# Copies moved, v's weights joined, key sums halved and TensorE kept busy at the start of an attention and FFN layer

## The chip, the cores and the metric

The kernel runs on one NeuronCore of a Trainium2 chip. The metric is the device time of one execution in microseconds. An engine is a unit of the core with an instruction queue of its own: TensorE (PE; its weight loads are PEld), VectorE (DVE), ScalarE (ACT), GpSimd (POOL), and SyncE (SP), which here only issues transfers. Transfers are also issued by POOL; those of POOL go into one queue and those of SP into another, and both are served by the same 16 DMA engines.

## The reference

```python
x = x + attn(layernorm(x))     # 2 x 2048 rows of 1024; one head of 256
x = x + ffn(layernorm(x))
# attn: q, k, v = x @ Wqkv + bqkv;  softmax(q k^T / 16) v;  @ Wo + bo
# ffn:  h = relu(x @ up_w) ** 2;  shared = h @ down_w
#       routed = ((x @ fc1_w) @ expert_w * (sum of the top 2 of x @ gate_w)) @ fc2_w
#       layernorm(shared + routed) * ln_gamma + ln_beta
```

up_w is 1024 x 2048, down_w 2048 x 1024, fc1_w 1024 x 512, expert_w 512 x 512, fc2_w 512 x 1024; all is fp32.

## The kernel before, in words

The 4096 rows are eight blocks of 512. Every fp32 operand of a product is split into a high and a low part, and a product is three matmuls: high x high, low x high, high x low. `Pass3` (line 130) issues them, so nearly all of TensorE's work has the line L130. A `split` (L142, L143) is a ScalarE copy for the high part and a VectorE (at times POOL) subtraction for the low part.

**Start** (`begin`, L458 and on). expert_w (tile `ew`) is loaded in four column pieces and transposed on TensorE (`pt`, L480); then fc2_w, the first rows of x and Wqkv are loaded by SP. expert_w and fc2_w are multiplied together once (`pf`, `fold`), in two halves; between the parts of the second half the first block's rows are transposed.

**Projections** (`qkv_block`, L408). For each block TensorE computes v in four tiles of 128 rows (`pv`, 3 x 8 matmuls of 256 columns each) and then q and k in four groups (`pq`, 24 matmuls of 512 columns). Blocks 4 to 7 come first, then 0 to 3. During a block the rows of the next one are normalised, transposed on VectorE within 32 x 32 squares (`xblk`, L213), written to memory (`xt_d`, L218) and fetched in another order (`xt`, L224), both by POOL, and split. The fourth tile is split by the next block (`x3`). q goes to memory (`q_d`), as k and v of blocks 4 to 7 do. The order here is the program's own (`manual_schedule`).

**Attention** (L715 to L775). In the loop over n, TensorE interleaves scores of block n (`ps`) with values of block n-1 (`po`). ScalarE copies scores out of PSUM, VectorE keeps their maximum; `row_max` transposes it; `softmax` subtracts, takes exp, splits, and adds each pair of key chunks into a tile `sum` of two halves of 512 columns. `finish` copies the output out (`o`) and sums over keys with one-column matmuls (`psum`, L622): two for each of four row tiles, which the profile counts as 16. `project` (L632) multiplies with Wo (`pw`) and adds the residual `xres`, which SP loads and to which POOL adds bo with an accumulating transfer (L638). A scheduler orders this part on each engine, and its order need not be the program's.

**FFN** (from L1033, in the program's own order). Each of four pairs of blocks runs an up stage (`pu`, with fc1_w beside up_w) and a down stage (`pd`, with the folded fc2 beside down_w), by a scheme of Strassen's kind: seven products p1 to p7 of quarters instead of eight, ten weight pieces each. The right factors are the quarters (0,0), (1,0), (1,1) of a weight matrix and four sums of quarters. `sum_step` (L387) makes them in memory by POOL's transfers during projections and attention: it copies the quarter, or the first term of a sum, and adds further terms with accumulating transfers. `stage`, `cast_piece` and `end_piece` load a piece (`w`, L810), make its high part on ScalarE (L833) and its low part on VectorE (L841), about two pieces ahead of TensorE; pieces that are used again are stored (`w_p`, L844). `Norm.step` normalises the second block of the first pair during the first up stage, group by group; `split_x` splits it for p4.

Of the kernel before, what the change touches and what calls it, by code (L numbers as in the profile page):

```python
# [17 lines left out]
P = 128  # L18
# [7 lines left out]
def kernel(  # L26
# [184 lines left out]
    def transpose_write(r, q=nc.gpsimd):  # L211
# [7 lines left out]
        return d  # L219

    def fetch_tile(d, q=nc.gpsimd):

        xt = row("xt")
        q.dma_start(  # L224
            out=xt.rearrange("p (a f) -> p a f", a=P // SQ),
            in_=d.rearrange("(a i) (q f) -> (i q) a f", i=SQ, q=P // SQ),
        )
        return xt
# [150 lines left out]


    FIRST = {1: (0, 1), 2: (1, 1), 3: (0, 1), 4: (1, 0)}
    SUMS = [(s, q) for s in range(2) for q in (1, 3, 2, 4)]
    COPIES = SUMS + [(s, q) for s in range(2) for q in ((0, 0), (1, 0), (1, 1))]
    ADDS = dict(zip((4, 5, 6, 8, 9, 10, 11, 13), SUMS))
    last = [None]

    def sum_step(i):  # L387

        s, q = COPIES[i]
        for o, t in zip(sum_tile(s, q), quarter(s, *FIRST.get(q, q))):  # L390
            nc.gpsimd.dma_start(out=o, in_=t)
        if i in ADDS:
            s, q = ADDS[i]
            if q % 2:
                terms = quarter(s, *((0, 0) if q == 1 else (1, 1)))
            else:
                terms = sum_tile(s, q // 2)
            for o, t in zip(sum_tile(s, q), terms):
                nc.gpsimd.dma_start(out=o, in_=t, accum_op=ALU.add, max_dma_last_dim=4096)

# [7 lines left out]
    def qkv_block(n, wqkv, xT, parts, after):  # L408

        keep = n < BPB
        units = {a: (unit if n == BPB - 1 else ex_unit)(f"{a}{n}") for a in "kv"}
        if keep:
            kv[n] = [units["k"], units["v"]]
        got = {}

        def v_tile(t):
            pm = bank(psa, "pv")
            if t % 2 == 0:  # L420
                got["v"] = half("v")
            acc = Pass3(pm[:, :D], NCC)
            for c in range(NCC):
                acc.add(x_chunk(xT, c, ts(t, P)), piece(wqkv[2], c, D, slice(0, D)))
            vt = got["v"][:, ts(t % 2, D)]
            nc.vector.tensor_tensor(vt, pm[:, :D], bv_sb, ALU.add)
            flush()
            split_late(vt, *(hl(units["v"])[:, s, ts(t, D)] for s in range(2)))

        def qk_chunk(a, dc):  # L430
            i = "qk".index(a)
            pm = bank(psa, "pq")
            acc = Pass3(pm, NCC)
            for c in range(NCC):
                acc.add(piece(wqkv[i], c, D, ts(dc, P)), x_chunk(xT, c))
            bias = bqk_sb[:, i * NDC + dc : i * NDC + dc + 1]
            flush()
            if a == "q":
                if dc == 0:
                    got["q"] = row("q")  # L440
                nc.scalar.activation(got["q"][:, ts(dc, W)], pm, AF.Identity, bias=bias)
            else:
                h, l = (hl(units[a])[:, s, ts(dc, W)] for s in range(2))
                nc.scalar.activation(h, pm, AF.Identity, bias=bias)
                nc.vector.scalar_tensor_tensor(l, pm, bias, f32(h), ALU.add, ALU.subtract)

        for j, (a, i) in enumerate(parts):
            v_tile(i) if a == "v" else qk_chunk(a, i)
            if (a, i) == ("q", NDC - 1):
                nc.gpsimd.dma_start(out=q_d[n], in_=got["q"])  # L450
            after(j)
        flush()
        if not keep:
            for a, d in (("k", k_d), ("v", v_d)):
                nc.gpsimd.dma_start(out=d[n], in_=f32(units[a]))

    order = list(range(BPB, NBLK)) + list(range(BPB))
    def begin(wqkv, xT):  # L458
# [15 lines left out]
        nc.gpsimd.dma_start(out=bv_sb, in_=bqkv[2 * D : 3 * D].partition_broadcast(P))  # L474

        eh, el = unit("eh"), unit("el")
        for mc in range(NLC):
            pt = bank(psc, "pt")
            for lc in range(NLC):
                nc.tensor.transpose(pt[:, ts(lc, P)], ew[:, ds(lc * LAT + mc * P, P)], ident)  # L480
            split(pt, eh[:, ts(mc, LAT)], el[:, ts(mc, LAT)])

        def split_f2(h, eng):
# [24 lines left out]
        for t in range(NB):  # L508
            if t + 1 < NB:
                stats.append(row_stats(first[t + 1]))  # L510
            normalise(first[t], stats[t])
            if t == 0:
                f2hl = split_f2(1, nc.gpsimd)
            elif t == 2:
                wqkv[2] = split_unit(*ws[2], nc.gpsimd)
        r = [folded(0, accs)]
        r.append(folded(1, fold(f2hl, lambda t: transpose_tile(first[t], t, xT))))
        wqkv[0] = split_unit(*ws[0])
# [48 lines left out]
    def row_max(n):  # L567
# [5 lines left out]
        m4 = small.tile([P, NB], FP, tag="m4", name="m4")  # L573
        nc.vector.tensor_reduce(m4, pt.rearrange("p (t k) -> p t k", k=P), AX.X, ALU.max)
        s["mb"] = bank(psc, "pmb")
        for t in range(NB):
# [4 lines left out]
    def softmax(n, j):  # L581
# [5 lines left out]
        e2 = e.rearrange("p (k n) -> p k n", n=W)  # L587
        mb = s["mb"].unsqueeze(1).to_broadcast([P, 2, W])
        nc.vector.tensor_tensor(e2, e2, mb, ALU.subtract)
        nc.scalar.activation(e, e, AF.Exp, scale=SC)  # L590
# [3 lines left out]
        elif j == 1:  # L594
            s["sum"] = row(f"sum{n}")
            nc.vector.tensor_tensor(s["sum"], s["e0"], e, ALU.add)
        else:
            nc.vector.tensor_tensor(s["sum"], s["sum"], e, ALU.add)

# [11 lines left out]
    def finish(n):  # L611
# [8 lines left out]
        for t in range(NB):  # L620
            for i in range(2):
                nc.tensor.matmul(  # L622
                    pt[:, t : t + 1],
                    lhsT=s["sum"][:, ds(i * W + t * P, P)],
                    rhs=ones,
                    start=i == 0,
                    stop=i == 1,
                )
        s["ri"] = small.tile([P, NB], FP, tag="ri", name="ri")
# [28 lines left out]
    def a_block(i, norm, xT, x3):  # L658
# [5 lines left out]
        def after(j):  # L664
            if i + 1 == NBLK:
                if j == 0:
                    x3()
                elif j == 2 * NB - 1:
                    start(0, load_row(q_d[0]))
                    for k in range(NKC):  # L670
                        scores(0, k)
                    start(1, load_row(q_d[1]))
                    row_max(0)
# [17 lines left out]
    wqkv, xT = {}, new_xT("a")  # L691
    with tc.manual_schedule():
        norm, fold = begin(wqkv, xT)
        x3 = lambda: None
        steps = list(range(len(COPIES)))
        for i in range(NBLK - 1):
            norm, xT, x3 = a_block(i, norm, xT, x3)
            if i == 0:
                for h in range(C // W):
                    nc.gpsimd.dma_start(  # L700
                        out=cols(fc2e, h, W), in_=fold[h].rearrange("p (c n) -> p c n", n=W)
                    )
            if i >= NBLK // 2:
                sum_step(steps.pop(0))
    a_block(NBLK - 1, None, xT, x3)

    wo_f = [load_row(Wo[ts(dc, P), :]) for dc in range(NDC)]

# [3 lines left out]
    for n in range(1, NBLK + 1):  # L712
# [4 lines left out]
        for k in range(NKC + lag):  # L717
# [23 lines left out]
            elif n == NBLK:  # L741
                if k < NB:
                    xts[k] = fetch_tile(xts[k], nc.sync)
                elif k % 2 == 0 and k >= 6 and k < 6 + 2 * NB:
                    split_x(xts, 0, k // 2 - 3, X["p1"])
            if k in (2, 8) and n > 1 and steps:
                with tc.issue_after(last[0].ins):
# [37 lines left out]

    UPS = [up_order(4 if b == 0 else 1) for b in range(NBLK // 2)]
    DOWN = [(p, i) for p in ("p1", "p2", "p6", "p5", "p3", "p7", "p4") for i in range(NK)]
# [4 lines left out]

    def source(s, q, i):
        t, j = (tsum[s, q][0], i) if i < HU // P else (tsum[s, q][1], i - HU // P)
        return t[:, ts(j, P)].rearrange("(c p) i -> p c i", p=P) if s == 0 else t[ts(j, P), :]

    def stage():
# [3 lines left out]
        if len(pieces) < LATE and early:  # L801
            staged.append((early.pop(0), False, None))
            return
        n_w[0] += 1
        w = (wk if n_w[0] % 7 else wv).tile([P, 2 * W], FR, tag="w", name="w")
        if (s, p, i) in kept:
            nc.sync.dma_start(out=w.bitcast(FP), in_=kept[s, p, i])
            staged.append((w, False, None))
            return
        nc.sync.dma_start(out=as_piece(f32(w)[:, W : 2 * W], s), in_=source(s, RIGHT[p], i))  # L810

# [4 lines left out]
        else:  # L816
            keep = b == 1 or i % 2 == 0
        staged.append((w, True, (s, p, i) if keep else None))

# [9 lines left out]
    def cast_piece():  # L829

        w, raw, key = staged.pop(0)
        if raw:
            nc.scalar.copy(w[:, 0:W], f32(w)[:, W : 2 * W])  # L833
        cast.append((w, raw, key))

    def end_piece():

        w, raw, key = cast.pop(0)
        if raw:
            v = f32(w)  # L840
            nc.vector.tensor_tensor(w[:, W : 2 * W], v[:, W : 2 * W], v[:, 0:W], ALU.subtract)  # L841
        if key:
# [190 lines left out]
    with tc.manual_schedule():  # L1033
        for b in range(NBB):
# [72 lines left out]
            for m, (p, i) in enumerate(UPS[b]):  # L1107
# [46 lines left out]
                if m % 2 and m < 17:  # L1154
                    out_step()
                if b == 0 and m in (0, 1, 2, 4, 6, 8, 9, 10, 11, 12, 13):
                    norm2.step()
                if b == 0 and m < NB:
                    split_x(x_t[0], 1, m, X["p2"], split_late)

                m4 = 12 if b == 0 else 10
                if m == m4:
# [174 lines left out]
```

## Time and profile before

| what | us |
|---|---|
| median of three runs | 2361.1 (2359.96 to 2361.95) |
| the profiled execution | 2357.94 |
| its span, from the first instruction to the last | 2355.8 |
| TensorE busy in the span | 2323.3 |
| VectorE busy | 1501.8 |
| ScalarE busy | 1168.1 |
| POOL busy | 285.4 |

The stages in the profiled execution: the start to 39 us, projections to 304, the first scores from there on, attention to about 776, then four pairs of up and down stages. The last matmul ends near 2342. Bytes moved are 572.54 MB in all.

In the page, a busy row gives tenths in 40 equal slices of the span, some 59 us each; PEclk is the TensorE clock granted, DMA the mean busy share of the 16 engines. A line of the chain of waits reads: start, duration, and what the time belongs to, with a count. A line of a timeline reads: start, duration, engine, line and operation, out<-in, shape and count, and in brackets the idle time before it with what ended it. Busy times of matmuls overlap, so their spacing is taken from the chain or from successive starts.

### The profile page before, as it was taken

The numbers are of one execution on the slowest core, as the hardware profiler recorded it, in microseconds if no ns is written. First come the engines' busy times: TensorE is split into PE (matmuls) and PEld (weight loads), VectorE is DVE, ScalarE is ACT, GpSimd is POOL, SyncE is SP. The second block draws the span as 40 slices with busy tenths as digits, with TensorE's granted clock in tenths as the row PEclk, the third lists the DMA queues.
The fourth block names the chain that finished last, engine by engine and source line by source line (L and its number), as shares of the span: only waits on it lengthen the run. The fifth ranks groups of instructions, "written<-read, shape, count | busy, mean of one in ns | idle before, by whom it ended". The sixth has DMA issues, their size and how long they took to land.

```text
span 2355.8 us, 29360 instructions
## 1 busy us (share of the span) xinstructions
PE 2323.3 (99%) x10704; PEld 1919.4 (81%) x10704; DVE 1501.8 (64%) x2238; ACT 1168.1 (50%) x1916; POOL 285.4 (12%) x425
## 2 busy tenths in 40 slices
PE   8999999999999999999999999999999999999997
PEld 7888888888887778788788888878888877888886
DVE  5566559888877575797645577753456683435656
ACT  6555455555544643667552374743055564214245
POOL 3232111011110110111110011110000021000001
PEclk9999999999999999999999999999999999999999
DMA  5977884999997766786897789786567589665674
GB/s 197 318 256 276 286 205 127 296 315 323 286 253 211 250 208 191 228 276 209 265 316 242 229 297 319 229 267 227 193 204 278 194 267 331 189 191 187 204 247 134
DMA packets 222208, 572.54 MB, mean 243 GB/s; under 512 B 18368, under 2 KB 80320, under 8 KB 220016
## 3 DMA queue, kind: packets, MB, share of 16 engines
q1 hardware_dynamic: 152160, 315.67, 39.9%
q0 software_dynamic: 69904, 255.00, 36.1%
q8 instruction: 85, 1.39, 0.2%
q14 instruction: 59, 0.48, 0.1%
HBM read 430.61 MB, written 197.66 MB: 267 GB/s over the span
## 4 chain that ended last, share of the span: by engine, by line
PE 91%; DMA 3%; issue 3%; DVE 1%; ACT 1%; POOL 0%; SPq 0%; POOLq 0%; DVEq 0%; ACTq 0%
PE pu L130 31%; PE pd L130 28%; PE po L130 7%; PE pq L130 7%; PE ps L130 7%; PE pv L130 4%; PE pw L130 4%; DMA w<-wt 2%; PE pg L890 1%; PE pf L130 1%; PE psum L622 1%; DMA xt<-xt_d 0%; DVE w L841 0%; DMA ew<-in_L_ffn_expert_w_dram 0%; DMA res<-x 0%
## 5 line engine op out<-in xcount | busy, mean ns | idle before, releaser
L130 PE MATMUL pd<-w,sp 128*128 128x512 f32 x3336 | 759.0, 389 | 4.9 <-DVE y L1274 4.8
L130 PEld LDWEIGHTS pd<-w,sp 128*128 128x128 f32 x3336 | 625.5, 188 | 137.3 <-ACT nm L260 6.0
L130 PE MATMUL pu<-xh,w 128*128 128x512 f32 x2240 | 692.8, 390 | 0.1
L130 PEld LDWEIGHTS pu<-xh,w 128*128 128x128 f32 x2240 | 419.2, 188 | 89.9 <-DVE w L841 1.5
L130 PE MATMUL pu<-xl,w 128*128 128x512 f32 x1120 | 436.2, 389 | 0.9 <-DVE xl L150 0.9
L841 DVE TENSOR_TENSOR w<-w 128x512 fp32r<-128x512 f32 x280 | 191.6, 687 | 99.0 <-ACT w L833 92.0
L833 ACT CAST w<-w 128x512 fp32r<-128x512 f32 x280 | 170.9, 615 | 166.2 <-DMA w<-wt 155.6
L130 PEld LDWEIGHTS pu<-xl,w 128*128 128x128 f32 x1120 | 210.2, 188 | 45.1 <-DVE xl L150 1.4
L1077 ACT CAST sp<-h 128x512 fp32r<-128x512 f32 x238 | 146.3, 618 | 151.9 <-PE pd L130 125.6
L1082 DVE TENSOR_TENSOR sp<-h,sp 128x512 fp32r<-128x512 f32 x238 | 162.9, 687 | 68.1 <-ACT sp L1077 67.9
L130 PE MATMUL po<-p,v 128*128 128x512 f32 x768 | 194.3, 391 | 0.6 <-DVE p L143 0.6
L130 PE MATMUL ps<-q,k 128*128 128x512 f32 x768 | 192.5, 390 | 1.5 <-DVE max L565 1.5
L130 PEld LDWEIGHTS ps<-q,k 128*128 128x128 f32 x768 | 143.6, 188 | 31.8 <-DVE max L565 1.9
L130 PEld LDWEIGHTS po<-p,v 128*128 128x128 f32 x768 | 143.0, 188 | 30.2 <-DVE p L143 1.0
L150 DVE TENSOR_TENSOR xl<-xt,xh 128x512 fp32r<-128x512 f32 x108 | 74.4, 689 | 134.9 <-ACT xh L149 134.9
L1027 ACT ACTIVATE h<-h 128x1024 f32<-128x1024 f32 x48 | 50.7, 1055 | 208.8 <-DVE h L1137 159.8
L560 ACT COPY s<-ps 128x512 f32<-128x512 f32 x128 | 75.0, 587 | 133.5 <-PE ps L130 133.4
L213 DVE STREAM_TRANSPOSE xblk<-xrow 128x1024 f32<-128x1024 f32 x60 | 121.1, 2018 | 9.6 <-ACT xrow L283 9.6
L844 POOL DMA_DIRECT2D w_p<-w x115 | 61.6, 536 | 508.7 <-DVE w L841 435.0
L565 DVE TENSOR_TENSOR max<-ps,max 128x512 f32<-128x512 f32 x120 | 82.4, 687 | 36.3 <-ACT s L560 36.1
L130 PE MATMUL pq<-xha,w_h 128*128 128x512 f32 x256 | 99.7, 389 | 0.0
L130 PE MATMUL pq<-xha,w_l 128*128 128x512 f32 x256 | 99.7, 389 | 0.0
(181 smaller groups left out, 3031.8 us busy)
## 6 DMA issues: line engine op xcount, KB each, us to landing
w<-w_p SPq DMA_DIRECT2D x280, 512.0 KB, 4.2
w<-wt SPq DMA_DIRECT2D x280, 256.0 KB, 3.4
w_p<-w POOLq DMA_DIRECT2D x115, 512.0 KB, 4.6
xt_d<-xblk POOLq DMA_DIRECT2D x56, 512.0 KB, 4.4
xt<-xt_d POOLq DMA_DIRECT2D x56, 512.0 KB, 6.7
wt<-in_L_ffn_up_w_dram POOLq DMA_DIRECT2D x9, 2048.0 KB, 23.8
wt<-in_L_ffn_down_w_dram POOLq DMA_DIRECT2D x9, 2048.0 KB, 31.1
xres<-in_L_attn_x_dram SPq DMA_DIRECT2D x32, 512.0 KB, 11.2
```

The costliest lines, as they stand in the source:

```text
L130: nc.tensor.matmul(self.ps, lhsT=a, rhs=b, start=self.i == 0, stop=self.i == self.n - 1, skip_group_check=self.on,)
L150: late_ops.append(lambda: nc.vector.tensor_tensor(lo, t, f32(hi), ALU.subtract))
L213: nc.vector.transpose(b.rearrange("p (q k i) -> p q k i", q=P // SQ, i=SQ), r.rearrange("p (k i q) -> p q k i", k=NCC, i=SQ),)
L560: nc.scalar.copy(s["s"][k // 4][:, ts(k % 4, W)], pm)
L565: nc.vector.tensor_tensor(s["max"], pm, s["max"], ALU.max)
L622: nc.tensor.matmul(pt[:, t : t + 1], lhsT=s["sum"][:, ds(i * W + t * P, P)], rhs=ones, start=i == 0, stop=i == 1,)
L833: nc.scalar.copy(w[:, 0:W], f32(w)[:, W : 2 * W])
L841: nc.vector.tensor_tensor(w[:, W : 2 * W], v[:, W : 2 * W], v[:, 0:W], ALU.subtract)
L844: nc.gpsimd.dma_start(out=kept[key], in_=w.bitcast(FP))
L1027: nc.scalar.activation(o, v, AF.Relu)
L1077: nc.scalar.copy(t[:, 0:W], v)
L1082: add(t[:, W : 2 * W], v, f32(t)[:, 0:W], ALU.subtract)
```

## The change

- `v_tile`: the high and low parts of v's weights lie side by side in one tile, so the high part of x is multiplied with both in one matmul of 512 columns, and the low part of x with the high part in one of 256. VectorE adds the two halves of the result. `begin` splits these weights in two parts, later than before.
- `softmax`: ahead of the last pair of key chunks the two halves of `sum` are added, and the last pair is added in two steps of 512; `finish` then needs one matmul for each row tile.
- `begin`: 3, 14 and 5 transposes of the identity into a spare bank, before, amid and after the transposes of expert_w.
- `sum_step`: only sums are made in it, with the steps in a new order (17 of them, a copy and an addition each a step). One step is issued in `begin`, one after block 4 of the projections (i == 4), three after the maximum of attention block 0 (behind a small POOL addition that reads it), the others two for each n from 2 to 7. The down stage's plain quarters are copied by `copy_step`: (0,0) after i == 5, (1,0) and (1,1) in 20 pieces during the first up stage. The up stage's plain quarters are read from up_w and fc1_w directly into another buffer (`raw`), except for the first four pieces, of which a copy `lead` is made.
- Loads of the first two q rows and of Wo go from SP's queue to POOL's, behind the last fetch of the projections.
- In the first up stage the second block's normalisation runs at m = 0, 1, 2, 3, 4, 6, 7, 8, 9, 10, 11 (before: 0, 1, 2, 4, 6, 8 to 13), and its split starts at m = 11 instead of 13.

```diff
+    FIRST = {1: (0, 1), 2: (1, 1), 3: (0, 1), 4: (1, 0)}
+    SECOND = {1: (0, 0), 2: 1, 3: (1, 1), 4: 2}
     SUMS = [(s, q) for s in range(2) for q in (1, 3, 2, 4)]
-    COPIES = SUMS + [(s, q) for s in range(2) for q in ((0, 0), (1, 0), (1, 1))]
-    ADDS = dict(zip((4, 5, 6, 8, 9, 10, 11, 13), SUMS))
+    STEPS = [(a, 0) for a in SUMS[:3]]
+    for a, c in zip(SUMS, SUMS[3:] + [None] * 3):
+        STEPS += ([(c, 0)] if c else []) + [(a, 1)]
+    STEPS.insert(3, None)
...
+    def copy_step(q, part=None):
+
+        for j, (o, t) in enumerate(zip(sum_tile(1, q), quarter(1, *q))):
+            if part is None:
+                nc.gpsimd.dma_start(out=o, in_=t)
+            elif part // (HU // P) == j:
+                i = ts(part % (HU // P), P)
+                nc.gpsimd.dma_start(out=o[i, :], in_=t[i, :])
...
-                acc.add(x_chunk(xT, c, ts(t, P)), piece(wqkv[2], c, D, slice(0, D)))
+                xh, xl = x_chunk(xT, c, ts(t, P))
+                w = wqkv[2][c // 4].rearrange("p (c n) -> p c n", n=2 * D)[:, c % 4]
+                ops = [(pm, xh, w), (pm[:, :D], xl, w[:, :D])]
...
+            nc.vector.tensor_tensor(vt, pm[:, D : 2 * D], vt, ALU.add)
...
+        busy(3)
         for mc in range(NLC):
+            if mc == 2:
+                busy(14)
...
+        busy(5)
...
+        if n == 0:
+
+            mark = small.tile([P, NB], FP, tag="mark", name="mark")
+            after = nc.gpsimd.tensor_tensor(mark, m4, m4, ALU.add)
+            with tc.issue_after(after.ins):
+                for _ in range(3):
+                    sum_step(steps.pop(0))
...
+        if last:
+            half_sum = s["sum"][:, 0:W]
+            nc.vector.tensor_tensor(half_sum, half_sum, s["sum"][:, W:C], ALU.add)
...
+            for i in range(2):
+                nc.vector.tensor_tensor(half_sum, half_sum, e[:, ts(i, W)], ALU.add)
...
+    with tc.issue_after(fetched[0].ins):
+        q_rows = [load_row(q_d[i], nc.gpsimd) for i in range(2)]
     a_block(NBLK - 1, None, xT, x3)
 
-    wo_f = [load_row(Wo[ts(dc, P), :]) for dc in range(NDC)]
+    with tc.issue_after(fetched[0].ins):
+        wo_f = [load_row(Wo[ts(dc, P), :], nc.gpsimd) for dc in range(NDC)]
...
+    def direct(s, p, i):
+
+        return s == 0 and p in ("p1", "p2", "p3") and (p, i // LEAD) != ("p1", 0)
...
+        if direct(s, p, i):
+            raw = spp.tile([P, 2 * W], FP, tag="sp", name="raw")[:, 0:W]
+        else:
+            raw = f32(w)[:, W : 2 * W]
+        nc.sync.dma_start(out=as_piece(raw, s), in_=source(s, p, i))
...
-                if b == 0 and m in (0, 1, 2, 4, 6, 8, 9, 10, 11, 12, 13):
+                if b == 0 and m in (0, 1, 2, 3, 4, 6, 7, 8, 9, 10, 11):
                     norm2.step()
...
-                m4 = 12 if b == 0 else 10
+                if b == 0 and m % 2 == 0 and 14 <= m < 14 + 4 * NK:
+                    j = m // 2 - 7
+                    copy_step((1, j // NK), j % NK)
+
+                m4 = 10
```

## The prediction

> **What bounds the kernel now.** I read the page first, to see which engine has no slack.
>
> ```profile
> span 2355.8 us, 29360 instructions
> ...
> PE 2323.3 (99%) x10704; PEld 1919.4 (81%) x10704; DVE 1501.8 (64%) x2238; ACT 1168.1 (50%) x1916; POOL 285.4 (12%) x425
> ...
> PEclk9999999999999999999999999999999999999999
> DMA  5977884999997766786897789786567589665674
> ```
>
> TensorE is busy 99% of the span; everything else has slack on average, though DMA stands at 9 from slice 7 to 11, the attention stage. So the time is the sum of TensorE's spacings plus its few gaps, and an edit counts by what it does to one or the other. The spacing of matmuls comes from the chain of waits, which here is TensorE itself:
>
> ```profile
> 39.43 11.51 PE pv L130 x96
> 50.94 21.79 PE pq L130 x96
> ...
> 378.89 1.68 PE psum L622 x16
> ```
>
> A v group of 256 columns follows its predecessor by 11.51/96 = 120 ns, a q/k group of 512 by 21.79/96 = 227 ns, a one-column sum over keys by 1.68/16 = 105 ns. Then the gaps: in the order of TensorE's starts I looked for every step longer than its kind's usual one. The start first (timeline of TensorE):
>
> ```profile
> 3.67 1.94 PE L480 MATMUL pt<-ident,ew 128*128 128x128 f32 x8 [3.67 <-DMA ew<-in_L_ffn_expert_w_dram]
> 9.11 1.94 PE L480 MATMUL pt<-ident,ew 128*128 128x128 f32 x8 [3.49 <-DMA ew<-in_L_ffn_expert_w_dram]
> 12.24 0.79 PE L130 MATMUL pf<-f2h,eh 128*128 128x512 f32 x1 [1.19 <-ACT f2h L142]
> ```
>
> Seven starts from 12.24 on lie about 427 ns apart instead of 227; only at 15.57 does the clock record show the full clock. The largest gap is at the last block of the projections (chain of waits, 266 to 282 us):
>
> ```profile
> 268.85 1.69 issue
> 270.54 7.66 DMA xt<-xt_d
> ...
> 278.23 0.63 ACT xha L142
> ```
>
> The last transposed tile lands at 278.2 and TensorE, at its v group, loses 2.39 + 0.86 = 3.25 us; the clock record then shows half clock from 281.81 for 3.41 us, another 1.6 us. The other gaps: 1.65 us at 712 and 1.09 us at 832; three of 1.3 to 2.2 us at the ends of the down stages (1138, 1530, 1922) and the 13 us after the last matmul, which the change leaves alone. The one at 712 starts here (timeline of ScalarE):
>
> ```profile
> 705.64 0.59 ACT L560 COPY s<-ps 128x512 f32<-128x512 f32 x1 [2.13 <-PE ps L130]
> 711.90 0.62 ACT L833 CAST w<-w 128x512 fp32r<-128x512 f32 x1 [5.66 <-DMA w<-wt]
> ```
>
> ScalarE stands 5.66 us for the first FFN weights, the score copies queue behind it, and a score group waits for its bank.
>
> **The change part by part**, against the profiled execution's 2357.94 us (span 2355.8, 2.1 around it). The median of the runs, 2361.1, is 3.2 above that; I take the difference to the median.
>
> *v's weights side by side.* Per tile and chunk three groups of 256 (3 x 120 = 360 ns) become one of 512 and one of 256 (227 + 120 = 347). 8 blocks x 4 tiles x 8 chunks = 256 times 13 ns = **-3.3 us**, all on the path. The Trainium skill ("TensorE: Matmul & The Clock Gate", Back-to-back issue gap) speaks against it: warm spacing is columns/2.4 plus only 2.5 ns, so joining two groups would save 256 x 2.5 = 0.6 us. The rows show 2 x 120 - 227 = 13 ns of fixed cost per group in this kernel, and I take the rows. VectorE gets 32 more additions of 128x256 from PSUM, 0.42 us each by the v row (13.4 us in eight 33 us blocks in which it is some 60% busy): hidden under TensorE; a v bank is held 0.4 us longer of four, 2.8 us apart: nothing. Without that cover it would be 13 us. The hi and lo halves of the v weights now come from two POOL subtractions of half size (4.62 us by the row at 26.59, so 2.3 each), ending near 34, before the first v group near 36.5: nothing.
>
> *Sums over keys halved.* 8 of 16 one-column passes per finish go: 8 blocks x 8 x 105 ns = 6.7 us. That time also covered the copies of the attention output that the projection needs. In the finishes at 378 to 666, VectorE's chain itself waits 1.2 us for these sums, so it moves up with them, and TensorE has five to seven score groups in between: full gain. At 725 the second half of the output ends at 727.3 and is needed at 727.4; there I give back 0.4. **-6.3 us**. VectorE pays three additions of 512 (0.69 each) for one of 1024 (1.2) per block, +0.9 of 57 us at 83% load: hidden, and not in the last stretch before the sums.
>
> *Kept awake.* 3 + 14 + 5 transposes of the identity. At 243 ns cold (1.94/8) the 14 fill 3.4 of the 3.49 us before 9.11. TensorE is then busy from about 3 to 12, so it should be at full clock at 12.2: the cold excess of 0.37 + 6 x 0.20 = 1.57 us goes, and the last eight transposes take 109 instead of 243 ns, of which the landing of the last weights and VectorE's first low half leave some 0.4. **-2.0 us**. Ends: 0 if such transposes don't count as activity, -2.6 if nothing else is late. The skill's same page (Part 1) says the clock follows free-running windows of some 3.4 us; the record agrees (281.81 and 15.57 are 78 x 3.413 us apart), so the cold stretch of an unprofiled run can be longer than this one, and the gain with it.
>
> *Loads of the last block.* Today SP starts two q rows at 261.7 and 264.1 and the two Wo rows at 270.0, beside the last writes and fetches of tiles; the last write takes 8.0 us and the last fetch 7.7, against 5.1 and 4.4 one block earlier. The change puts these four loads behind the last fetch on POOL's queue; what then stands behind them there is the q store and the gate weights, wanted much later (q's first use is near 298). With the earlier durations the last tile lands near 272, and it is wanted at 278: the 3.25 us and the half-clock stretch go. **-4.6 us** (ends 0 and -4.9). The 2.5 MB copy ahead of that block stays, now of a down quarter; in the block before, the same sort of copy cost no TensorE time.
>
> *Terms where transfers idle.* The first copy moves to about 33 us, when SP's loads have landed; before the first tile write near 50 it has 16 us, and a 2.5 MB copy took 15.7. Three more steps (6 MB) move behind the maximum of block 0, near 336, where DMA is 0.34 busy from 340 to 380. In the six blocks after it 4 copies and 8 additions remain instead of 11 and 8. The weights at 705 then share the queue with less: an idle start gave 2.8 us for the same size (ew's first landing at 3.54), so ScalarE waits some 3 us less: **-1.3 us** of the 1.65. The direct reads of up_w are as large and in runs as short (512 B) as those from the copies; ScalarE's and VectorE's work per piece is the same: nothing. 20 pieces of 256 KB go into the first up stage, 10 MB of traffic in some 110 us at 0.6 to 0.7 DMA load; weights are taken two pieces (5.4 us) ahead and land in 3.4: nothing. POOL issues them behind stores of weights, about 0.6 us each, and nobody waits: nothing. On POOL the first copy's two issues (1.3 us) stand ahead of the low half of k's weights, which waits 12.5 us for ScalarE anyway. Raw pieces, from the fifth on, land in buffers that lie where v's units lay, so SP's fifth load waits for the last reads of v (near 752 today), and behind it on SP the stores of the last block's output, first wanted at 767: nothing.
>
> *Second tile set of the first up stage two groups earlier.* The 1.09 us at 832 (low half of x not ready) goes. But ScalarE now gets four tiles' moments (1.45 + 1.65 + 1.25 us each) in 11 groups with two fewer pauses: added up from group 2, its work runs 9 us behind at group 7, today 6 us, and today's slack at 812 was 0.2 us. Between -1.1 and +3; I take **-0.5**.
>
> Sum: -3.3 - 6.3 - 2.0 - 4.6 - 1.3 - 0.5 = -18.0; 2357.9 becomes 2339.9, the median 2361.1 becomes 2343.
>
> **Rivals.** *The residuals come late (slower).* The 6 MB at 336 now stand ahead of the four bo additions of block 0's output (issued at 302 to 315 today), and these wait besides behind the marker that waits for the maximum. 5 MB took 26.7 us at 316, so 6 MB end near 371 and the first residual near 374, when VectorE wants it at 383.7. At the fullest rate, 10 MB in 53 us from 407, it is 32 us: the same. Past four banks (5.4 us) every microsecond more is one of TensorE; to be slower than before, 6 MB would need some 65 us. A delay beyond 18 us gives 2362 to 2366. *The cover of the sums is lost* at all eight finishes: 2349. *ScalarE overload* in the up stage: +3 to +6, 2347 to 2349. *It doesn't do what it says*: transposes don't wake the clock, or the down copy, in runs of 2 KB, keeps the last fetch late: 2345 to 2350.
>
> **How the numbers follow.** About 0.2% (4.7 us) is what a measurement of this kernel can tell from no change. As summed (2340 to 2346.5): 0.70. Cover lost: 0.06. Overload: 0.09. Not as said: 0.09. Two of these together or something unseen, within 0.2%: 0.02. Residuals late and slower: 0.04. Faster 0.94, same 0.02, slower 0.04. The range, 2338 to 2351, takes in the first four and the ends of the unknown costs.
>
> **What would show it.** v chunks 347 ns apart; psum x8 per finish in 0.84 us; full clock at or before 12.2; no DMA step near 270 and no half clock near 280; no ScalarE wait over 3 us at the first w cast; no gap at the first p4 group, or one earlier. Wrong if VectorE waits for xres at block 0's projection, or pw for o.

## The result, and the profile after

The kernel after takes 2347.3 us (median of 4 executions, 2347.24 to 2350.12), the kernel before 2360.5 us beside it (4 executions, 2359.26 to 2361.95). The ratio is 0.9948, with a 95% interval of 0.9936 to 0.996. So the change gains 13.2 us where the forecast said 18. The profiled execution took 2347.36 us, with a span of 2345.6: 10.6 us below the profiled execution of before, which itself lay 2.6 us under its median.

The page of the kernel after, against the lines shown of before:

```profile
span 2345.6 us, 28754 instructions
...
PE 2316.7 (99%) x10406; PEld 1897.6 (81%) x10406; DVE 1518.9 (65%) x2286; ACT 1167.9 (50%) x1917; POOL 291.5 (12%) x442
...
PEclk9999999999999999999999999999999999999999
DMA  7868749799977777686897688786668589555684
```

TensorE is still the bound, with 298 matmuls fewer. The span fell by 10.2 us and TensorE's busy time by 6.6; the rest, 3.6, was idle time of TensorE. In the row of DMA the sixth and seventh slice, 293 to 410 us, went from 8 and 4 to 4 and 9: there the steps behind the maximum of block 0 now run. Of the five nines of attention, the eighth to twelfth slice (7 to 11 where the prediction counts from nought), two became sevens. The slices of the first up stage, the fourteenth to seventeenth, went from 7 6 6 7 to 7 7 7 6.

Where the span went shows in the first start of each stage on TensorE, taken from the two traces (us from the span's start):

| first start of | before | after | difference so far | of this stage |
|---|---|---|---|---|
| v groups, block 0 | 39.27 | 38.44 | -0.83 | start: -0.83 |
| score groups | 310.49 | 305.53 | -4.96 | projections: -4.13 |
| first down stage | 974.27 | 963.40 | -10.87 | attention and first up stage: -5.91 |
| the last matmul | 2342.16 | 2332.39 | -9.77 | the rest: +1.10 |
| end of span | 2355.8 | 2345.6 | -10.2 | after the last matmul: -0.4 |

So the projections of the kernel before run to 310 us, and not to 304 as the list of its stages has it.

The chain of waits in the kernel after gives the spacings (start, duration, what; each line out of its own stretch):

```profile
38.60 11.28 PE pv L446 x64
49.88 10.21 PE pq L130 x45
...
373.83 0.79 PE psum L687 x8
```

A v chunk takes 11.28/32 = 352 ns, where the three groups took 360: 7.5 ns less, somewhat over half of the 13 that I had counted on. The sums over keys take 0.79 us per finish instead of 1.68.

The start, in the timeline of TensorE:

```profile
5.57 1.86 PE L510 MATMUL busy<-ident 128*128 128x128 f32 x14
9.21 0.63 PE L519 MATMUL pt<-ident,ew 128*128 128x128 f32 x4 [1.78 <-DMA ew<-in_L_ffn_expert_w_dram]
...
11.86 0.50 PE L130 MATMUL pf<-f2h,eh 128*128 128x512 f32 x1 [0.65 <-ACT f2h L142]
12.20 0.39 PE L130 MATMUL pf<-f2h,el 128*128 128x512 f32 x1
```

The clock record shows full clock from 5.91 on, and the transposes at 9.21 and the first fold run at the full rate. The last block of the projections, in the chain of waits, is now TensorE alone:

```profile
262.00 10.65 PE pq L130 x47
272.65 11.28 PE pv L446 x64
283.93 6.12 PE pq L130 x27
```

No transfer stands in it any more, and from 281 to 286 the granted clock is 1.00 (0.66 before). ScalarE's first cast of FFN weights waits 2.39 us, not 5.66 (its timeline):

```profile
698.30 0.62 ACT L912 CAST w<-w 128x512 fp32r<-128x512 f32 x1 [2.39 <-DMA w<-wt_lead]
```

and the step of 1.65 us near 712 is gone. Two things are new, both losses. In the projections, steps of 0.2 to 1.0 us near 104, 122, 155, 238 and 255 us, 2.7 us more between 100 and 300 than in the trace of before (the last block's step left out). And in the first up stage TensorE loses 4.8 us from 750 to 850 instead of 2.2 (spacings beyond the usual one of their kind, summed over the trace's starts). Its largest step is 2.35 us at 814. The chain of waits there:

```profile
794.36 5.78 DMA xt<-xt_d
...
801.41 0.69 DVE w L919
802.11 0.02 SPq L889
...
802.16 10.21 DMA raw<-in_L_ffn_fc_w_dram
...
812.45 0.62 ACT w L912
...
815.80 0.69 DVE w L919
...
816.54 10.99 PE pu L130 x47
```

It reads: VectorE's subtraction ends; that frees a raw buffer; SP issues the next direct read; it takes 10.2 us; ScalarE casts, VectorE subtracts, TensorE goes on. L919 is the line that frees the buffer, and L889 the load.

### The profile page after: what moved, and what is told of

Same layout as the page of the kernel before. It is cut to its first block, busy times and chain, and to the rows that moved or that the text cites. A ratio compares the mean times of both kernels' runs of the same rounds, so it can differ in the third digit from the quotient of the medians.

```text
span 2345.6 us, 28754 instructions
## 1 busy us (share of the span) xinstructions
PE 2316.7 (99%) x10406; PEld 1897.6 (81%) x10406; DVE 1518.9 (65%) x2286; ACT 1167.9 (50%) x1917; POOL 291.5 (12%) x442
## 4 chain that ended last, share of the span: by engine, by line
PE 84%; DMA 5%; issue 4%; DVE 4%; ACT 2%; POOL 1%; SPq 0%; POOLq 0%; DVEq 0%; ACTq 0%
PE pu L130 31%; PE pd L130 28%; PE po L130 7%; PE ps L130 7%; PE pw L130 4%; PE pq L130 3%; DMA xt_d<-xblk 2%; DMA w<-wt 2%; PE pv L446 1%; PE pg L968 1%; DVE xblk L213 1%; DVE xla L143 1%; DMA w<-in_L_attn_Wqkv_dram 1%; DMA raw<-in_L_ffn_fc_w_dram 0%; PE pf L130 0%
## 5 line engine op out<-in xcount | busy, mean ns | idle before, releaser
L912 ACT CAST w<-w 128x512 fp32r<-128x512 f32 x241 | 147.2, 616 | 134.4 <-DMA w<-wt 124.5
L919 DVE TENSOR_TENSOR w<-w 128x512 fp32r<-128x512 f32 x241 | 164.6, 685 | 69.6 <-ACT w L912 67.0
L130 PE MATMUL pq<-xla,w_h 128*128 128x512 f32 x256 | 99.7, 389 | 0.0
```

The costliest lines, as they stand in the source:

```text
L130: nc.tensor.matmul(self.ps, lhsT=a, rhs=b, start=self.i == 0, stop=self.i == self.n - 1, skip_group_check=self.on,)
L912: nc.scalar.copy(w[:, 0:W], raw)
L919: nc.vector.tensor_tensor(w[:, W : 2 * W], raw, f32(w)[:, 0:W], ALU.subtract)
```

## The experiments

Times are medians, each with its ratio to the kernel before on the same chip. The kernel after stands at 2347.3 us, 0.9948 (0.9936 to 0.996).

**The norm of the first up stage back in its old groups.**

```
-if b == 0 and m in (0, 1, 2, 3, 4, 6, 7, 8, 9, 10, 11):
+if b == 0 and m in (0, 1, 2, 4, 6, 8, 9, 10, 11, 12, 13):
...
-m4 = 10
+m4 = 12 if b == 0 else 10
```

> The kernel after, with only the second norm of the first up stage put back to the groups that it had before, and its x switched at group 12 instead of 10. Theory A, the earlier norm is what costs: the profiled first up stage of the kernel after has a step of 0.86 us at 773.6 (TensorE waits for ScalarE, which stands behind the moments) and one of 2.35 us at 814.0 (ScalarE waited 4.6 us for two direct reads that took 10.4 us beside tile fetches issued at 794 to 803). With the old places both go, 3.2 us, and the 1.1 us step near 832 of the kernel before returns: about 2 us less than after, near 2345.3. Rival B, the direct reads or the copy pieces are slow whatever the norm does: the long ScalarE wait stays near 810, time within 0.7 us of after or up to 1 us more.

Measured: 2348.5 us, 0.9949 (0.9935 to 0.9963). My first theory fell. The step of 0.86 us went, and the one of 1.1 us near 822 came back, but the large one did not go: it is 3.19 us at 812, and half clock follows it (0.50 from 816.9 to 820.3). Two direct reads issued at 800.78 and 801.94 took 10.7 and 10.4 us here too. The norm's place isn't the cause of the large step.

**Without the transposes of the identity.**

```
-busy(3)
...
-    if mc == 2:
-        busy(14)
...
-busy(5)
```

> The kernel after without its 22 transposes of the identity. Theory A, the clock part works but most of its gain is lost again to the second fold, where VectorE and GpSimd wait for the loads: by the profiles the first pv started 0.83 us earlier, so about 0.8 us more than after, near 2348.1. Rival B, the gain of 2.0 that I forecast: 2349.3. Rival C, without a profile the clock's windows fall otherwise and the cold stretch is longer: 2.5 us or more, 2350 or above, although its profile shows less.

Measured: 2349.2 us, 0.9953 (0.9941 to 0.9966), 1.8 us more than after, with intervals that overlap. The timeline of TensorE:

```profile
8.82 1.94 PE L516 MATMUL pt<-ident,ew 128*128 128x128 f32 x8 [2.96 <-DMA ew<-in_L_ffn_expert_w_dram]
11.95 0.79 PE L130 MATMUL pf<-f2h,eh 128*128 128x512 f32 x1 [1.19 <-ACT f2h L142]
12.54 0.63 PE L130 MATMUL pf<-f2h,el 128*128 128x512 f32 x1
```

Here the clock is full only from 17.24 on, not from 15.57 as in the profile of before: the cold stretch of the fold is 5.3 us long instead of 3.3. From the last eight ew transposes to the first v group it takes 31.1 us, in the kernel after 29.2, before 30.2. So the part is worth 1.9 us beside this execution and 0.9 beside the one profiled before. The difference of 1.8 us is nearest to the second expectation, but with its interval it agrees with any of the three.

**v's three groups apart again.**

```
-ops = [(pm, xh, w), (pm[:, :D], xl, w[:, :D])]
...
+acc.add(x_chunk(xT, c, ts(t, P)), (w[:, :D], w[:, D:]))
...
-nc.vector.tensor_tensor(vt, pm[:, D : 2 * D], vt, ALU.add)
```

> The kernel after with v's three groups of 256 columns per chunk again and without the second VectorE addition; the weights stay side by side in memory. Theory A: joining gained 256 x 7.5 ns = 1.9 us of TensorE spacing, and the second addition (four of 0.42 us per block) lengthened the chain of VectorE transposes, tile writes and fetches by which new stalls of 2.2 us together came into the projections at 104, 122, 155, 238 and 255 us. So those stalls go and the spacing comes back: within 0.7 us of after. Rival B, the stalls come from elsewhere (moved copies and loads): they stay, and the time is 1.9 to 3.3 us more.

Measured: 2347.4 us, 0.9946 (0.9934 to 0.9959): no difference. In its trace no step of the projections from 50 to 300 us is longer than its kind's usual one, and v's starts are 120 ns apart again. So this part of the change gives 1.9 us and takes about as much: theory A.

**The sums over keys at full width.**

```
-half_sum = s["sum"][:, 0:W]
-nc.vector.tensor_tensor(half_sum, half_sum, s["sum"][:, W:C], ALU.add)
...
+for i in range(2):
+    nc.tensor.matmul(
...
+        lhsT=s["sum"][:, ds(i * W + t * P, P)],
```

> The kernel after with the sums over keys of 1024 columns again, 16 one-column products per finish. Theory A, their cover was not needed: 7 us more by the profiles (13.6 against 6.5 us of psum steps), near 2354.3. Rival B, part of the time was taken back by waits for the output of attention that now come sooner: under 5 us more.

Measured: 2354.9 us, 0.9979 (0.9971 to 0.9988), 7.5 us more than after. In its chain of waits the finish of block 0 reads as before:

```profile
372.86 1.68 PE psum L684 x16
```

Over eight finishes the psum steps take 13.61 us here and 6.46 in the kernel after, and in neither does TensorE wait at the projections that follow. The cover was not needed.

**The four loads of the last block on SP again.**

```
-q_rows = [load_row(q_d[i], nc.gpsimd) for i in range(2)]
...
+start(0, load_row(q_d[0]))
...
-wo_f = [load_row(Wo[ts(dc, P), :], nc.gpsimd) for dc in range(NDC)]
+wo_f = [load_row(Wo[ts(dc, P), :]) for dc in range(NDC)]
```

> The kernel after with only the two q rows and the two Wo rows of the last projection block loaded on SP's queue again, where they stood before. Theory A, these loads are what made the last fetch of a tile late: the step near 270 to 278 of 3.25 us and the 1.6 us of half clock behind it come back, 4.8 us more, near 2352. Rival B, the other copy in this place (a quarter of the down weights in place of the term copies) made the room, and the loads alone are worth under 2 us: below 2349.3.

Measured: 2355.2 us, 0.9977 (0.9967 to 0.9987), 7.8 us more than after: theory A in kind, and larger in size. The chain of waits:

```profile
272.04 7.65 DMA xt<-xt_d
279.69 0.02 issue
279.71 0.63 ACT xha L142
```

These are nearly the lines of the kernel before. The last write of a tile takes 7.1 us from its issue to its landing and the last fetch 7.7, in the kernel after 4.5 and 4.7. The steps add up to 5.2 us here (3.25 before) and two stretches of half clock follow instead of one: from 250 to 300 TensorE loses 7.7 us, in the kernel after 0.3. The up stage adds 1.9 us in this profile, since half clock follows the step at 821 that the kernel after has at 814.

**Two direct reads in one raw buffer.** The raw tile had 1024 columns, of which a read used 512.

```
-raw = spp.tile([P, 2 * W], FP, tag="sp", name="raw")[:, 0:W]
+if n_raw[0] % 2 == 0:
+    pair_raw[0] = spp.tile([P, 2 * W], FP, tag="sp", name="raw")
+raw = pair_raw[0][:, ts(n_raw[0] % 2, W)]
+n_raw[0] += 1
```

> The kernel after, but two direct reads share one raw buffer of 1024 columns, of which they used half: eight places instead of four in the same four buffers. Theory A, formed after the norm was put back and the stall stayed: in the first up stage SP's queue waits for VectorE to free a raw buffer (32 us in 11 waits from 760 to 815), so the reads are issued only some 10 us ahead of their use, and when four tile fetches and weight stores make one read take 10 us, TensorE runs dry. With eight places the reads are issued earlier: the 2.35 us step at 814 and the half clock that follows it in other profiles go, 2.3 us less than after or more, near 2345. Rival B, the traffic alone is the cause: the step stays and the time is within 0.7 us of after.

Measured: 2342.9 us, 0.9931 (0.9919 to 0.9942), the best of all, 4.4 us below after. SP's waits from 760 to 815 us, first in the kernel after, then here (who waited for whom: us in total, times, the longest):

```profile
SPq L889 <- DVE w L919: 32.3, 11, 5.1
SPq L889 <- DMA w_p<-w: 8.1, 2, 6.1
```

```profile
SPq L892 <- DVE w L923: 23.1, 4, 7.7
SPq L892 <- DMA w_p<-w: 15.0, 2, 13.7
```

SP still waits for VectorE, but four times and not eleven, since it has eight places to run ahead in. SP waited in the kernel before as well, but mostly for TensorE (the same stage, 775 to 830 us):

```profile
SPq L810 <- PE pu L130: 20.8, 10, 4.1
```

So the sum of the waits doesn't tell the difference; what does is how far ahead of ScalarE's cast a read leaves. For the direct reads that leave from 780 us on this is 6 to 13 us in the kernel after and 12 to 20 here; for the loads of the kernel before in the same place (783 to 813 us) it is 11 to 16. A load of 9.3 us, issued at 812.5, cost TensorE nothing in the kernel before: it had left 11.3 us ahead. The last two direct reads leave here at 792.7 and 793.1, and not at 802.2 and 802.7, where three fetches of tiles and two stores of weights are under way. The chain of waits shows what that is worth:

```profile
795.99 27.27 PE pu L130 x119
```

TensorE runs from 796 to 823 without a wait; the step at 814 is gone. Theory A stands, and the traffic alone is not the cause: the same fetches and stores are made. The size is less sure than the cause. The two profiled executions differ by 5.0 us, of which the attention and the first up stage make 2.6; the rest lies in stages in which the two kernels do the same (0.5 at the start, 1.2 in the projections, 0.6 behind the first up stage).

**v joined, without the second addition.**

```
-nc.vector.tensor_tensor(vt, pm[:, D : 2 * D], vt, ALU.add)
```

> The kernel after with v's joined products, but without the second VectorE addition of each v tile (so v lacks the product of x's high half with the weights' low half). Theory A, the addition is what lengthens the projections' chain: the new stalls at 104, 238, 255 and near 276 go while the joined spacing stays, about 2 us less than after, near 2345.3. Rival B, the stalls come because TensorE's block became shorter than the chain of tile writes and fetches, with or without the addition: they stay, within 0.7 us of after.

Measured: 2344.3 us, 0.9934 (0.9922 to 0.9946), 3.0 us below after. The chain of waits of the kernel after, where the step at 104 lies, and then of this one:

```profile
93.14 9.98 DMA xt_d<-xblk x2
...
103.22 1.27 ACT q L471 x2
104.48 0.52 ACT xha L142
...
110.04 0.34 DVE v L455
...
110.41 0.43 DVE v L456
...
118.05 2.03 DVE xblk L213
```

```profile
94.97 9.97 PE pq L130 x44
104.94 11.28 PE pv L446 x64
116.22 8.85 PE pq L130 x39
```

With the addition (L456) the chain goes through VectorE's transposes, the tile writes, ScalarE's q, which waits for a row buffer that such a write still reads, and the split of x. Without it the chain is TensorE alone, and no step is left from 50 to 300 us, though the block is just as short. The three groups apart, which have no second addition either, had no step there. So the addition is the cause, and not the shorter block: theory A.

**v's low half by GpSimd.**

```
+late_ops.append(lambda: eng.tensor_tensor(lo, t, f32(hi), ALU.subtract))
...
-split_late(vt, *(hl(units["v"])[:, s, ts(t, D)] for s in range(2)))
+split_late(vt, *(hl(units["v"])[:, s, ts(t, D)] for s in range(2)), nc.gpsimd)
```

> The kernel after with the subtraction for the low half of v (four per block of 0.41 us on VectorE) made by GpSimd. This gives VectorE back what the second addition takes. Theory A, VectorE's place in the chain decides: the stalls in the projections go, about 2 us less than after, near 2345.3. Rival B, GpSimd's queue, on which the tile writes and fetches are issued, is delayed by more than VectorE gains: the stalls stay or grow, 2347.3 or up to 3 us more.

Measured: 2347.1 us, 0.9948 (0.9936 to 0.996), executions from 2344.8 to 2350.1: undecided. Its profile (span 2343.4) has one step of 0.46 us left in the projections; the step at 811 in the up stage stays.

**Both together.**

```
+raw = pair_raw[0][:, ts(n_raw[0] % 2, W)]
...
+split_late(vt, *(hl(units["v"])[:, s, ts(t, D)] for s in range(2)), nc.gpsimd)
```

> Two raw reads per buffer and v's low half by GpSimd together, in the kernel after. Theory: the two causes are separate, the raw buffers (4.4 us measured) and VectorE's place in the projections' chain (stalls of 1.2 us left in the profile of the kernel with paired reads, of 2.2 in after): about 1 us less than with paired reads alone, near 2341.8, faster than both kernels. Rival: GpSimd's subtractions cost as much as they give, 2342.9 or more.

Measured: 2345.6 us, 0.9942 (0.993 to 0.9955). The rival holds: no gain over paired reads alone. In its profile the projections have two steps, 0.54 and 0.88 us, the larger one at the end of this chain of waits:

```profile
183.32 2.03 DVE xblk L213
185.35 1.18 DVE st L178 x2
...
187.31 0.42 DVE v L456
...
187.88 4.33 PE pq L130 x18
```

VectorE is still the link. The up stage stays mended (2.5 us lost from 750 to 850), but the ends of two down stages lost 2.9 and 2.7 us against 1.8 and 1.9 with paired reads alone.

**Paired reads, norm in its old groups.**

```
+raw = pair_raw[0][:, ts(n_raw[0] % 2, W)]
...
+if b == 0 and m in (0, 1, 2, 4, 6, 8, 9, 10, 11, 12, 13):
...
+m4 = 12 if b == 0 else 10
```

> Paired raw reads in the kernel after, with the second norm of the first up stage at its old groups. With the raw reads out of the way this prices the moved norm by itself. Theory A: the step of 0.86 us at 772 goes and the one of 1.1 us near 822 (low half of x not ready) returns, so within 0.7 us of paired reads alone (2342.9). Rival B, the earlier norm gained the 0.5 or more that I forecast: 2343.4 to 2344. Rival C, it cost: below 2342.2.

Measured: 2345.4 us, 0.994 (0.9927 to 0.9954). That is above every expectation, but the surplus isn't in the stage that was changed: from 750 to 850 TensorE loses 2.0 us, with the norm early 2.1. Its projections lost 3.5 us in this profile (1.2 with paired reads alone), and nothing there differs between the two kernels. So by the profiles the norm's move is worth about nothing (the medians differ by 2.5 us, with intervals that overlap): it exchanges the 0.86 us step at 772 for the one of 1.1 us near 819, whose release the chain of waits shows:

```profile
802.28 16.40 PE pu L130 x71
...
819.32 0.69 DVE xl L150
...
820.05 5.07 PE pu L130 x21
```

**Paired reads, GpSimd, and the norm in between.**

```
+raw = pair_raw[0][:, ts(n_raw[0] % 2, W)]
...
+split_late(vt, *(hl(units["v"])[:, s, ts(t, D)] for s in range(2)), nc.gpsimd)
...
+if b == 0 and m in (0, 1, 2, 4, 6, 7, 8, 9, 10, 11, 12):
...
+m4 = 11 if b == 0 else 10
```

> As e9 (paired reads, v's low half by GpSimd), with the second norm's steps at groups 0, 1, 2, 4, 6 to 12 and its x switched at group 11. Theory: ScalarE's backlog at group 3 is relieved, so the 0.86 us step near 771 goes, and x comes one group later than in after, so of the 1.1 us step near 822 at most half returns: 0.3 to 0.9 us less than e9. Rival: one of the two steps is as large as ever, within 0.3 us of e9.

Measured: 2345.6 us, 0.9942 (0.993 to 0.9955), level with the one without it. The 0.86 us step at 771 went, and steps of 0.59, 0.26 and 0.41 us came between 796 and 800. The rival holds.

**The same two without the transposes of the identity.**

```
+raw = pair_raw[0][:, ts(n_raw[0] % 2, W)]
...
+split_late(vt, *(hl(units["v"])[:, s, ts(t, D)] for s in range(2)), nc.gpsimd)
...
-busy(3)
...
-    if mc == 2:
-        busy(14)
...
-busy(5)
```

> As e9 without the 22 transposes of the identity: the awake part priced where the first up stage no longer scatters the runs. Theory A, TensorE's first v group starts about 1.2 us later, as in the profiles (39.9 against 38.4 to 38.9 us): 1.2 us more than e9, within 0.6. Rival B: the 2.0 of my forecast or more, as the first comparison (1.8) suggests.

Measured: 2345.5 us, 0.9942 (0.993 to 0.9955), 0.1 us less than with them: neither expectation. Its trace does show the loss: 31.4 us from the last ew transposes to the first v group, against 29.0. But those transposes ran at 7.9 us here and at 8.4 there; over all the profiles the last landing of ew moves their start from 7.9 to 9.8 us. That spread is as large as the effect.

## Why the prediction was right, and where its terms were off

The time lies inside the range, and the direction and the two largest terms, the sums over keys and the loads, are right, but the sum was 18.0 and 13.2 came. The two traces account for 10.2 of it: 7.15 less for the sums over keys, 4.5 for the last block, 1.5 in the rest of attention, 0.8 at the start and 0.4 behind the last matmul; 0.5 more for v with its new steps, 2.6 in the first up stage and 1.1 behind it. Another 0.4 lies outside the spans, and 2.6 is what the profiled execution of before lies under its median, which no trace explains. That the time still lies inside the range owes something to luck: the four terms that missed by more than 1 us (the start, v, the up stage, what lies behind it) were all too hopeful, and the 2.6 us came from no term.

*Sums over keys*, -6.3. Right: the psum steps fell by 7.15 us in the trace and putting the sums back cost 7.5. The 0.4 I gave back at 725 was not lost: TensorE has no wait from 700 to 760 us in the kernel after.

*Loads of the last block*, -4.6. Right: 250 to 300 us loses 0.3 instead of 4.8 us, half clock included; undoing the loads alone cost 7.8, of which its profile shows 7.4 there. It was the place of the loads, and not the other copy, that mattered.

*Terms moved*, -1.3. The step at 712 went, 1.5 us with its surroundings. Which of the moved copies did it wasn't tried singly, so this cause is argued and not shown.

*Kept awake*, -2.0. The mechanism is right: full clock from 5.91, and a first fold without a cold stretch. The profiled gain up to the first v group is 0.83, since what is late next is GpSimd's low half of the second fold's weights (four subtractions without a gap from 21.19 to 27.13, after their input had landed at 20.46, 0.56 us later than before) and then VectorE's low half of x, which TensorE awaits for 0.6 us at 27.2. Taking the transposes out showed 1.9 to 2.4 us in two traces, and +1.8 and -0.1 us in two comparisons of medians. The size stays open between nothing and 2.

*v side by side*, -3.3. The failed steps are the term and its cover. The term: the "347" per chunk was 352, because the 512-column group is followed after 235 and not 227 ns, so 256 x 7.5 ns = 1.9 us. The rule of the Trainium skill ("TensorE: Matmul & The Clock Gate", Back-to-back issue gap) gave an estimate of 0.6, the row 3.3; the measurement lies between. The page gives that rule for an isolated matmul and says that in a stream the weight loads set the spacing as well, so it was used beyond its reach: the measured 227 and 120 ns are each some 11 ns above it. The cover: "32 more additions ... hidden under TensorE" was wrong. I compared VectorE's load with the block's length, some 60%, and did not follow the chain through it. The transposes of the next block's tiles wait behind these additions in VectorE's order, and from there go the tile write, the row buffer that ScalarE's q waits for, and the next x. Steps of 0.6 to 3.5 us together came in the profiles with the addition (that with the loads on SP left out); in the two without it there were none. Net of this part: nothing that the medians can tell.

*Direct reads of the up weights*, nothing. This is the step that failed most. The sentence that "weights are taken two pieces (5.4 us) ahead" looked at the order of the issues and not at the buffers. From a copy, a weight landed in its own w tile; a direct read lands in one of four raw buffers, which VectorE's subtraction frees. I had named the place of these buffers, and only asked who held them before. With them SP stands 32 us in 11 waits for VectorE, and the reads are pushed into the time of the fetches. Eight profiles with single reads lose 4.3 to 8.0 us from 750 to 850, five with paired reads 2.0 to 2.5, the one before 2.2. That is +2.6 us in the profile after, which has no half clock there and lies at its kernel's median, and up to 5.8 where half clock follows the step. The 4.4 us between the medians of the kernel after and of paired reads also holds what the other stages of those executions differ by.

*Norm earlier*, -0.5. The 1.09 us at 832 went as said, and the ScalarE backlog that I feared came as 0.86 us at 773.6. Net: nothing, by the profiles with paired reads.

*Residuals late*, the slower rival. It didn't come: the four bo additions landed at 357 to 365 us, and VectorE's waits from 366 to 385 are for the maximum (1.1 us) and for TensorE (0.9), none for a residual.

Not foreseen: the ends of the down stages, +1.1 us after the first up stage. They vary by themselves, from 1.4 to 4.0 us (the latter with a stretch of half clock) at the same place over the profiles, so I put no cause to that.

The best version tried is the kernel after with paired raw reads, 0.9931 (0.9919 to 0.9942) of before. It beats the kernel before beyond its interval, and the one after by its median; their intervals against before just overlap. The four kernels with paired reads and one or two further edits all stand at 2345.4 to 2345.6, so its 2342.9 may be at the lucky end. That v apart and paired reads together would do as well, with less work on VectorE, was not tried.

## What to carry to other kernels

When a load gets another landing place, ask who frees that place and how many there are: the depth of the run ahead is set by the buffers, not by the order of the issues. A busy share of 60% is no cover for work that is put ahead of a step on which the next tile depends; follow that tile through each engine's queue. Work taken from the bounding engine itself (the sums over keys) came in whole; the losses lay where an edit gave another engine or buffer more to do.

## What the runs showed of the hardware that I had not expected

- A 512-column group followed by one of 256 takes 235 ns, and the 256 after it 117.5; among their own kind they take 227 and 120. The saving of joining two groups was 7.5 ns, not 13.
- The clock's full rate came at 5.9 to 11.1 us with the transposes of the identity and at 15.6 to 17.2 without. The stretches of half clock within the work were 3.41 us, or two of them in a row (6.83 us, after 5.2 us of steps). Between two changes of the clock there lay whole multiples of 3.413 us: 78, 1 and 604 in the profile of before, 79, 2, 157, 1 and 445 in that with the loads on SP. The length of a step alone did not decide: one of 2.83 us (at 1515, paired reads and GpSimd) was followed by no half clock, one of 2.14 us (at 1518, the same with the norm in between) was.
- A 256 KB read of weights that took 2.7 us at its quickest took 10.2 to 10.7 when four to eight other transfers were open on the two queues.
